# Causal attention, first sequence: keys' parts in tiles of their own, four heads' rows written and two pairs loaded ahead of the rest

## The chip, the cores and the metric

One kernel, one launch, on one core of a Trainium2 chip. The metric is the device time of that launch in microseconds (us), taken as the median over several runs. The time before is 2537.52 us, the median of five runs between 2535.51 and 2549.70 us.

## The reference, cut to what matters

The program is a stack of layers on `x` of shape (4, 1024, 128): a gated linear attention, a mixture of experts, a causal softmax attention, a second mixture of experts, a rotary linear attention with a dense network, a softmax attention with a slope per head ("alibi"), and a dense network again. The change sits in the causal attention:

```
q = (x @ Wq).reshape(B, T, 16, 8).transpose(0, 2, 1, 3)      # B = 4, T = 1024
k = (x @ Wk).reshape(B, T, 16, 8).transpose(0, 2, 1, 3)
v = (x @ Wv).reshape(B, T, 16, 64).transpose(0, 2, 1, 3)
scores = einsum('bhqd,bhkd->bhqk', q, k) / sqrt(8)
scores = where(causal, -inf, scores)
ctx = einsum('bhqk,bhkd->bhqd', softmax(scores), v)
out = ctx.transpose(0, 2, 1, 3).reshape(B, T, 1024) @ Wo
```

`x` has been layer-normed before, and `out` is added to `x`.

## The kernel before

**Pairs.** Heads are worked on two at a time; a sequence has 16 heads, so 8 pairs, and the four sequences have 32. Queries and keys are each split into a high part `hi`, rounded to the matmul's fp32r format, and the remainder `lo`. One product over four copies of the 8 channels (hi.hi, hi.lo, lo.hi, lo.lo) then gives nearly full precision. To bring these copies onto the right partitions they go through device memory: `Pairs.lay_out` writes four copies `a = 0..3` of a whole sequence's queries (`which` 0) or keys (`which` 1) into an image, 16 heads x 8 channels x 1024 positions, 512 KB for each copy (L702). For the queries, copies 0 and 1 are `hi`, 2 and 3 are `lo`; for the keys, 0 and 2 are `hi`, 1 and 3 are `lo`. `Pairs.load` then reads the rows of one pair back, 32 rows of 4 KB for each head, four transfers of 128 KB: two of queries, two of keys (L711). Tiles for six pairs are held. All of these transfers are issued by SyncE (SP), in the order in which they stand in its program. They take one of eight completion semaphores in turn, so that a transfer waits for the eighth before it to have landed.

**Prologue of a sequence** (`prologue(b)`): the experts' result is added to `x`, layer norm, transposes (`xnT`), then for queries and keys in turn: two matmuls of 512 columns into banks of PSUM (L903), a rounding copy to `hi` on ScalarE (L904), the subtraction to `lo` on VectorE (L905), and `lay_out`. `hi` and `lo` are single buffers, so the keys' parts are made in the place of the queries' parts once the queries' rows have left. For the first sequence it also makes the first values `v` (`values`, matmuls L921, copies L927). For later sequences the prologue runs in the middle of the attention of the one before.

**Maxima.** For each pair, `maxima` makes all scores once with the queries stationary (TensorE, L722, `bank<-ca_k,ca_q`; 24 products of 128 to 512 columns) and finds the greatest of each row on VectorE (L750 with the causal mask, L755 without). The maxima are turned (L764), split, and put into the queries' tile as two more rows for each head by small transfers (L772), 8 rows of 512 B each. These pieces are handed out by an iterator `ahead`: 30 pieces, that is two and a half pairs, stand before the first exponential, and later ones are mixed in.

**Main loop** (`softmax_attention`): for two pairs at a time, over blocks of keys: the scores again, with the keys stationary (L722, `scores<-ca_q,ca_k`), the mask added by two small matmuls for each head (`hide`, L728), the exponential on ScalarE (L853) into a tile `e` or, for the first block, `e_first`; then the products with the values (L972, `o<-e,v`), and the sum of exponentials on GpSimd (L990). There is one PSUM buffer for the scores. The tiles `e` are a pool of four buffers of 128 x 1024 words.

**Order.** The order of each engine's instructions is set when the program is built, by a scheduler which works with estimates of its own; on the chip each engine takes its instructions in that order. `alibi_front`, the prologue of the later attention, uses the same `lay_out`; there the rounding copies are L1107 on ScalarE and the subtractions L1108 on GpSimd.

Of the kernel before, what the change touches and what calls it, by code (L numbers as in the profile page):

```python
# [13 lines left out]
F32 = mybir.dt.float32  # L14
I32 = mybir.dt.int32
F32R = mybir.dt.float32r
# [4 lines left out]
P = 128  # L21
B, T = 4, 1024
NB = T // P
NT = B * NB
H = 16
DK = P // H
# [612 lines left out]
class Pairs:  # L639
# [54 lines left out]
            base=512 - P, channel_multiplier=1,  # L694
        )

    def lay_out(self, b, which, hi, lo):

        rows = self.images[b % 2][which][:, self.at :, :].rearrange("h (d a) t -> h d a t", a=4)
        for a in range(4):  # L700
            part = (lo if a >= 2 else hi) if which == 0 else (lo if a % 2 else hi)
            self.k.nc.sync.dma_start(rows[:, :, a, :], part.bitcast(F32))  # L702

    def load(self, n):

# [80 lines left out]
def softmax_attention(  # L786
    k: Core, pairs: Pairs, work, ps_e, scale, maxima, prologue, consume, hold, beside, before=lambda b: None,
    begun=False,
):

    nc = k.nc
    per = H // 2
    count = B * per

    def all_maxima():  # L800
        finish = None
        for n in range(count):
            pieces = maxima(n)
            next(pieces)
            yield
            if finish is not None:
                finish()
            finish = yield from pieces
        finish()

    ahead = all_maxima()
    later = deque()

    def some(n=1):
        for _ in range(min(n, len(later))):
            later.popleft()()

    turn = 0

    if not begun:  # L820
        prologue(0)
        for n in range(4):
            pairs.load(n)

    for _ in range(len(BY_QUERY) * 2 + 6):
        next(ahead, None)
    late = None
    for first in range(0, count, 2):
        if first % per == 0 and first // per + 1 < B:
            before(first // per + 1)  # L830
        if first % per == 2 and first // per + 1 < B:
            prologue(first // per + 1)
        for n in (first + 4, first + 5):
            if n < count:
                pairs.load(n)
        for c, j in BY_KEY:
            start = max(j * P, c * 512)
            w = (c + 1) * 512 - start
            es = []
            for i in range(2):  # L840
                n = first + i
                ps = ps_e.tile([P, 2, 512], F32, tag="scores", name="scores")
                for g in range(2):
                    pairs.product(
                        ps[:, g, :w], n, g, slice(start, start + w), slice(j * P, (j + 1) * P), "k", True,
                        j < 4 * c,
                    )
                if j >= 4 * c:
                    for g in range(2):
                        pairs.hide(ps[:, g, :P], g)  # L850
                tag = "e_first" if hold and j == 0 else "e"
                e = work.tile([P, 2, 512], F32, tag=tag, name=tag)
                power = nc.scalar.activation(e[:, :, :w], ps[:, :, :w], AF.Exp, scale=scale)  # L853
                k.mark = [power.ins.name]
                es.append(e)
                next(ahead, None)
                if late is not None:
                    later.extend(late[i]() or ())
                some()
                turn += 1  # L860
                if beside and turn % 3 == 0:
                    beside.popleft()()
            late = consume(first // per, first % per // 2, c, j, es)
    for part in late:
        later.extend(part() or ())
    some(len(later))
    while beside:
        beside.popleft()()
    next(ahead, None)


def causal_attention(k: Core, pairs: Pairs, wq_d, wk_d, wv_d, wo_d, bring, after):
# [5 lines left out]
    with (  # L878
# [14 lines left out]
        def prologue(b):  # L893
            got.pop()()
            xnT = k.normed(two, b, 1)
            normal[b] = xnT
            for which, w in enumerate((wq, wk)):
                hi = two.tile([P, T], F32R, tag="hi", name="hi", bufs=1)
                lo = two.tile([P, T], F32R, tag="lo", name="lo", bufs=1)
                for c in range(2):  # L900
                    cut = slice(c * 512, (c + 1) * 512)
                    ps = k.bank()
                    nc.tensor.matmul(ps, lhsT=w, rhs=xnT[:, cut], start=True, stop=True)  # L903
                    nc.scalar.copy(hi[:, cut], ps)  # L904
                    nc.vector.tensor_sub(lo[:, cut], ps, hi[:, cut].bitcast(F32))  # L905
                pairs.lay_out(b, which, hi, lo)
            if b == 0:
                for piece in values(b, 0):
                    piece()

# [2 lines left out]
        def values(b, r):  # L913

            v = two.tile([P, NB, 4, dv], F32, tag="v", name="v")
            held[b, r] = v

            def piece(t):
                ps = k.bank()
                for i in range(2):  # L920
                    nc.tensor.matmul(  # L921
                        ps[:, i * 256 : (i + 1) * 256],
                        lhsT=normal[b][:, (t + i) * P : (t + i + 1) * P],
                        rhs=wv[:, r * 256 : (r + 1) * 256],
                        start=True, stop=True,
                    )
                nc.scalar.copy(v[:, t : t + 2].rearrange("p t h d -> p (t h d)"), ps)  # L927

            return [partial(piece, t) for t in range(0, NB, 2)]
# [27 lines left out]
        def consume(b, r, c, j, es):  # L957
# [68 lines left out]
            return first, second  # L1026

        softmax_attention(
            k, pairs, work, ps_e, 1.0 / math.sqrt(DK), partial(pairs.maxima, pool=two, steps=BY_QUERY),
            prologue, consume, True, beside, lambda b: got.append(bring(two, b, "got")),  # L1030
        )

# [93 lines left out]
def alibi_attention(k: Core, pairs: Pairs, weights: AlibiWeights):  # L1126
# [3 lines left out]
    with (  # L1130
# [54 lines left out]
        def consume(b, r, c, j, es):  # L1185
# [53 lines left out]
            return lambda: None, second  # L1239

        softmax_attention(
            k, pairs, work, ps_e, 1.0, partial(pairs.maxima, pool=two, steps=BY_QUERY), prologue, consume,
            False, deque(), begun=True,
# [538 lines left out]
```

## Time and profile before

| | |
|---|---|
| median of five runs | 2537.52 us (2535.51 to 2549.70) |
| the profiled execution's own time | 2543.76 us |
| its span | 2542.0 us |
| mean granted TensorE clock | 0.919 |
| TensorE busy | 2250.7 us, 89% of the span |
| VectorE, ScalarE, GpSimd busy | 1663.7, 1252.6, 926.9 us |
| causal attention | from about 296 to about 1190 us |
| first prologue: addition of the experts' result to first product for the maxima | 300.22 to 331.96 us |

The page has shares of the whole span. For one place in it the order of time has to be read: the timeline gives a start, a duration, engine, line, operation and output and input tiles, a count of merged instructions, and in brackets the idle time before and what ended it. The windows give, for a stretch of time, the busy time of each engine with its count of instructions, then the granted TensorE clock, the busy share of the 16 DMA engines, and GB/s. A matmul in fp32 is recorded twice.

### The profile page before, as it was taken

To read this page: it belongs to the slowest core of one execution; us is meant where nothing else is said; L and a number is where in the kernel's file an instruction comes from. 1 tells how busy PE (TensorE), PEld (TensorE's weight loads), DVE (VectorE), ACT (ScalarE), POOL (GpSimd) and SP (SyncE) were. 2 spreads that over 40 slices of the span, in tenths; PEclk is the share of its full clock that TensorE was granted. 3 is DMA by queue.
4 is the path that set the end of the run, shared out by engine and by line. 5 is a ranking of instruction groups with operands and counts; after the bars stand their busy time and mean duration, and the time that the engine had idled before them with its cause. 6 is when DMAs were issued, how large, how long until landed. Compare 5 with 4: busy or idle time off the path is not lost. (4 is left out here: it accounts for less than half of the span.)

```text
span 2542.0 us, 39865 instructions
## 1 busy us (share of the span) xinstructions
PE 2250.7 (89%) x14101; PEld 1237.2 (49%) x14101; DVE 1663.7 (65%) x4795; ACT 1252.6 (49%) x2033; POOL 926.9 (36%) x722
## 2 busy tenths in 40 slices
PE   6885679999999999998985999989999999997998
PEld 4564533443434344443343666744445444444666
DVE  6978265767657765776434776477777767774544
ACT  6553214455444544553431566615555555556865
POOL 2213405677488748766762333311001000000222
PEclk8987769999889989998997999957999999998999
DMA  9300330200200120100033000402113131000000
GB/s 256 111 9 17 88 103 22 80 19 26 84 26 19 35 83 20 35 19 27 2 101 96 9 9 1 132 2 89 41 28 111 38 97 45 24 24 1 9 9 18
DMA packets 92391, 124.80 MB, mean 49 GB/s; under 512 B 13211, under 2 KB 66462, under 8 KB 92174
## 3 DMA queue, kind: packets, MB, share of 16 engines
q1 hardware_dynamic: 88862, 115.76, 16.2%
q0 software_dynamic: 2560, 5.30, 0.6%
q8 instruction: 120, 1.97, 0.3%
q10 hardware_dynamic: 752, 0.98, 0.1%
q14 instruction: 97, 0.79, 0.1%
HBM read 67.57 MB, written 52.85 MB: 47 GB/s over the span
## 5 line engine op out<-in xcount | busy, mean ns | idle before, releaser
L853 ACT ACTIVATE e<-scores 128x1024 f32<-128x1024 f32 (+3 forms) x704 | 544.8, 792 | 580.0 <-PE scores L728 289.0
L990 POOL TENSOR_TENSOR e_first<-e_first,e 128x1024 f32<-128x1024 f32 (+3 forms) x320 | 540.7, 1718 | 326.1 <-ACT e L853 260.5
L750 DVE CUSTOM_DVE_ANT_0 junk<-bank,mask 128x128 f32<-128x128 f32 (+3 forms) x1024 | 497.3, 486 | 200.4 <-PE bank L722 131.2
L755 DVE TENSOR_REDUCE nm<-bank 128x1 f32<-128x512 f32 x512 | 330.4, 681 | 146.8 <-PE bank L722 144.6
L972 PE MATMUL o<-e,v 128*32 128x512 f32 (+3 forms) x2560 | 305.0, 497 | 0.0
L722 PE MATMUL bank<-aa_k,aa_q 62*128 62x512 f32 (+3 forms) x768 | 245.1, 426 | 25.7 <-DVE nm L755 15.6
L722 PE MATMUL bank<-ca_k,ca_q 62*128 62x512 f32 (+3 forms) x768 | 190.8, 419 | 30.6 <-DMA ca_k<-ca_k 13.9
L1198 PE MATMUL o<-e,v 128*32 128x512 f32 (+3 forms) x1536 | 216.6, 512 | 0.0
L722 PE MATMUL scores<-ca_q,ca_k 64*128 64x512 f32 (+3 forms) x768 | 181.4, 444 | 28.4 <-ACT e L853 26.5
L722 PEld LDWEIGHTS scores<-ca_q,ca_k 64*128 64x128 f32 x768 | 78.2, 188 | 250.4 <-ACT e L853 158.6
L728 PE MATMUL scores<-halves 64*128 64x128 f32 x2048 | 198.8, 260 | 0.0
L728 PEld LDWEIGHTS scores<-halves 64*128 64x128 f32 x2048 | 191.8, 194 | 11.0 <-issue 3.9
L722 PE MATMUL scores<-aa_q,aa_k 64*128 64x512 f32 (+3 forms) x768 | 170.3, 411 | 4.9 <-ACT e L853 4.7
L722 PEld LDWEIGHTS bank<-aa_k,aa_q 62*128 62x128 f32 x768 | 119.1, 198 | 108.2 <-DVE nm L755 60.3
L1108 POOL TENSOR_TENSOR lo<-val,hi 128x512 fp32r<-128x512 f32 x16 | 20.2, 1277 | 388.6 <-ACT hi L1107 369.2
L1516 DVE TENSOR_TENSOR h<-val,h 128x512 fp32r<-128x512 f32 x128 | 90.9, 718 | 102.8 <-ACT h L1515 77.1
L1470 PE MATMUL bank<-h,ff_h1s 128*128 128x512 f32 x512 | 135.5, 409 | 15.4 <-POOL h L1464 10.5
L1460 POOL CAST h<-gate 128x512 fp32r<-128x512 f32 x32 | 26.6, 832 | 335.1 <-DVE gate L1493 325.5
L722 PEld LDWEIGHTS scores<-aa_q,aa_k 64*128 64x128 f32 x768 | 79.6, 190 | 137.9 <-ACT e L853 63.8
L1010 DVE RECIPROCAL raw<-raw 128x128 f32<-128x128 f32 x128 | 117.6, 936 | 44.2 <-ACT raw L1006 44.2
L722 PEld LDWEIGHTS bank<-ca_k,ca_q 62*128 62x128 f32 x768 | 94.7, 200 | 99.1 <-issue 39.2
L1510 ACT ACTIVATE val<-bank,ff_t 128x512 f32<-128x512 f32 x128 | 88.0, 689 | 84.5 <-PE bank L1470 74.6
(291 smaller groups left out, 3719.9 us busy)
## 6 DMA issues: line engine op xcount, KB each, us to landing
aa_q<-aa_q SPq DMA_DIRECT2D x64, 208.0 KB
ca_q<-ca_q SPq DMA_DIRECT2D x64, 128.0 KB
ca_k<-ca_k SPq DMA_DIRECT2D x64, 128.0 KB
aa_k<-aa_k SPq DMA_DIRECT2D x64, 128.0 KB
wi<-in_moe_wi_dram SPq DMA_DIRECT2D x16, 256.0 KB
wo<-in_moe_wo_dram SPq DMA_DIRECT2D x16, 256.0 KB
back<-blank SPq DMA_DIRECT2D x8, 512.0 KB
got<-back SPq DMA_DIRECT2D x8, 512.0 KB
```

The costliest lines, as they stand in the source:

```text
L722: self.k.nc.tensor.matmul(out, lhsT=lhsT, rhs=rhs, start=True, stop=stop, skip_group_check=True)
L728: self.k.nc.tensor.matmul(ps, lhsT=part[:, 0, :], rhs=part[:, 1, :], start=False, stop=(a == 1), skip_group_check=True,)
L750: nc.vector.tensor_tensor_reduce(junk[:, :cols], ps[:, :cols], self.mask[:, 512 - cols :], -1.0, 3e38, ALU.add, ALU.min, to,)
L755: nc.vector.tensor_reduce(to, ps[:, :cols], AX.X, ALU.max, negate=True)
L853: power = nc.scalar.activation(e[:, :, :w], ps[:, :, :w], AF.Exp, scale=scale)
L972: nc.tensor.matmul(outs[which][32 * i : 32 * i + 32, skip:], lhsT=v[:, j, i, 32 * which : 32 * which + 32], rhs=es[i // 2][:, i % 2, : 512 ...
L990: nc.gpsimd.tensor_add(to, to, es[i][:, :, : 512 - skip])
L1010: nc.vector.reciprocal(part, part)
L1198: nc.tensor.matmul(o[32 * i : 32 * i + 32, skip:], lhsT=v[:, j, 4 * r + i, :], rhs=es[i // 2][:, i % 2, : 512 - skip], start=(j == 0), sto ...
L1470: nc.tensor.matmul(ps, lhsT=weights[:, c, :], rhs=inputs[c][i], start=(s == 0), stop=(s == len(steps) - 1))
L1510: nc.scalar.activation(val, ps, AF.Gelu, scale=s[:, o : o + 1])
L1516: nc.vector.tensor_sub(nxt[1][:, o, :], val, hi.bitcast(F32))
```

## The change

For the first sequence, the keys' parts `hi` and `lo` are put into two tiles of the pool of exponentials instead of the buffers that hold the queries' parts. `lay_out` takes a range of heads. For the first sequence it is called four times: heads 0 to 3 of the queries, of the keys; then pairs 0 and 1 are loaded; then heads 4 to 15 of the queries and of the keys; then pairs 2 and 3 are loaded. The loads move from `softmax_attention` into the prologue, in front of the first values. And for the queries' copies, in every sequence and in both attentions, the order of writing becomes 0, 2, 1, 3 (`hi`, `lo`, `hi`, `lo`) instead of 0, 1, 2, 3.

```
-    def lay_out(self, b, which, hi, lo):
-        rows = self.images[b % 2][which][:, self.at :, :].rearrange("h (d a) t -> h d a t", a=4)
-        for a in range(4):
+    def lay_out(self, b, which, hi, lo, heads=slice(0, H)):
+        rows = self.images[b % 2][which][heads, self.at :, :].rearrange("h (d a) t -> h d a t", a=4)
+        of = slice(heads.start * DK, heads.stop * DK)
+        for a in (0, 1, 2, 3) if which else (0, 2, 1, 3):
             part = (lo if a >= 2 else hi) if which == 0 else (lo if a % 2 else hi)
-            self.k.nc.sync.dma_start(rows[:, :, a, :], part.bitcast(F32))
+            self.k.nc.sync.dma_start(rows[:, :, a, :], part.bitcast(F32)[of, :])
...
     if not begun:
         prologue(0)
-        for n in range(4):
-            pairs.load(n)
...
+            laid = []
             for which, w in enumerate((wq, wk)):
-                hi = two.tile([P, T], F32R, tag="hi", name="hi", bufs=1)
-                lo = two.tile([P, T], F32R, tag="lo", name="lo", bufs=1)
+                if b == 0 and which:
+                    hi, lo = (
+                        work.tile([P, 2, 512], F32, tag="e", name="e").bitcast(F32R).rearrange("p g q -> p (g q)")
+                        for _ in range(2)
+                    )
+                else:
+                    hi = two.tile([P, T], F32R, tag="hi", name="hi", bufs=1)
+                    lo = two.tile([P, T], F32R, tag="lo", name="lo", bufs=1)
...
-                pairs.lay_out(b, which, hi, lo)
+                if b:
+                    pairs.lay_out(b, which, hi, lo)
+                laid.append((which, hi, lo))
             if b == 0:
+                for part in laid:
+                    pairs.lay_out(b, *part, slice(0, 4))
+                for n in range(2):
+                    pairs.load(n)
+                for part in laid:
+                    pairs.lay_out(b, *part, slice(4, H))
+                for n in range(2, 4):
+                    pairs.load(n)
                 for piece in values(b, 0):
                     piece()
```

The built program's order changes with it. SP issues eight transfers of 128 KB, the loads of pairs 0 and 1, eight transfers of 384 KB, the loads of pairs 2 and 3. On ScalarE the keys' rounding copies stand before the copies of `v`. On TensorE the first scores (pair 0) and the first products with the values, which stood among the maxima of pairs 1 and 2, stand at the end of pair 2's maxima and behind them; some two hundred instructions on, both orders have done the same work. In the alibi attention's later prologues the keys' rounding copies stand one exponential later on ScalarE.

## Prediction

> **What bounds the kernel now.** The page's first part puts TensorE (PE) at 89% of the span, so time is lost where PE stands still or runs slowly. The change works on one such place, the start of the causal attention. Its timeline comes first (start, duration, engine, line, operation, tiles, count, idle time before and what ended it); lines of PE, ScalarE (ACT), VectorE (DVE) and SP's queue:
>
> ```profile
> 313.48 1.28 SPq L702 DMA_DIRECT2D ca_q<-hi  x2
> 314.80 3.06 SPq L702 DMA_DIRECT2D ca_q<-lo  x2
> ...
> 319.28 1.07 ACT L904 CAST hi<-bank 128x512 fp32r<-128x512 f32 x2 [0.57 <-DMA ca_q<-hi]
> 320.37 1.16 SPq L702 DMA_DIRECT2D ca_k<-hi  x2
> 322.43 1.29 DVE L905 TENSOR_TENSOR lo<-bank,hi 128x512 fp32r<-128x512 f32 x2 [8.25 <-DMA ca_q<-lo]
> 323.75 1.16 SPq L702 DMA_DIRECT2D ca_k<-lo  x2
> 325.11 2.69 SPq L711 DMA_DIRECT2D ca_q<-ca_q  x2
> 329.59 0.77 SPq L711 DMA_DIRECT2D ca_k<-ca_k  x2
> ...
> 331.96 7.44 PE L722 MATMUL bank<-ca_k,ca_q 62*128 62x128 f32 x14 [13.88 <-DMA ca_k<-ca_k]
> ```
>
> The keys' parts wait for the queries' buffers, the keys' load waits for the last row written, and PE waits 13.88 us. This is what the change attacks. The second view is the windows (length; busy us and count of PE, PEld, DVE, ACT, POOL; then granted clock, DMA share, GB/s): first a stretch of the writing, then the idle stretch and what follows.
>
> ```profile
> 315.00:319.00 4.00, 3.08 (x14) 2.12 (x13) 0.00 (x0) 2.34 (x4) 0.00 (x0) 1.00 1.00 333
> ```
>
> ```profile
> 318.20:331.95 13.75, 0.00 (x0) 0.02 (x1) 1.29 (x2) 1.58 (x3) 0.00 (x0) 0.67 0.85 275
> 331.95:366.80 34.85, 31.42 (x70) 16.22 (x72) 29.10 (x101) 2.82 (x4) 0.00 (x0) 0.50 0.21 58
> 366.80:376.70 9.90, 8.82 (x35) 3.84 (x31) 7.41 (x23) 1.61 (x3) 0.00 (x0) 0.98 0.19 55
> 376.70:404.00 27.30, 27.30 (x164) 10.02 (x163) 12.69 (x37) 12.05 (x19) 11.70 (x8) 1.00 0.01 1
> ```
>
> The idle stretch costs twice: PE stands, and its clock then stays at 0.50 for the 35 us of the first maxima, in which DVE (29.10 busy) and the slow PE (31.42) share the pace. From 376.7 on PE has no gap at all, so whatever work is pushed behind that point adds to the end. The third view is the DMA's packets, in a stretch in which the four 512 KB queries' writes landed, and one in which two of the 8-row writes of L772 landed:
>
> ```profile
> DMA packets 665, 2.46 MB, mean 241 GB/s; under 512 B 64, under 2 KB 64, under 8 KB 665
> ```
>
> ```profile
> DMA packets 32, 0.01 MB, mean 3 GB/s; under 512 B 16, under 2 KB 32, under 8 KB 32
> ```
>
> Besides the data there are 64 tiny packets for four writes whose outermost count is 16 heads, so 16 each; and 16 for two writes of 8 rows, so 8 each. I read them as one closing packet for each DMA engine that took part: the outermost count, up to 16, sets how many share a write. A write of four heads would then use four engines.
>
> **The first rows (gain).** The first product for the maxima needs the queries' and keys' rows of pair 0. Both parts of the keys are now ready early: the keys' matmuls end at 314.55, two casts of 0.58 and two subtractions of 0.69 follow, about 316. SP puts out eight writes of 128 KB, 1.05 MB. Their speed is not in the trace, so I bound it. With all 16 engines at 333 GB/s they take 3.1 us, less than their issue: eight at about 0.6 (1.16 for two) from 313.48 give 318.3, plus some 2 us to land. The keys' load then needs, as before, 331.96 - 329.59 = 2.37 us: first product at 322.7, a gain of 9.2 us. With four engines, one engine moves 333/16 = 20.8 GB/s on average and 450/16 = 28 in the best slice (450 GB/s) of the same stretch, so four move 83 to 112 GB/s, and the eight take 9.4 to 12.6 us from the first bytes at about 314.6: 324.0 to 327.2, plus 0.3 to close and 2.37, first product at 326.7 to 329.9, a gain of 2.1 to 5.3. A row four times shorter on a quarter of the engines is no quicker; what is left is that the keys' rows no longer stop for the buffers. I take four engines, as 16 and 8 closing packets lie on that line, and the middle: 3.7 us.
>
> The Trainium skill ("DMA: Bandwidth & Descriptors", section "Why a DMA increments its semaphore by 16 and not by 1") speaks against this change in the same way: the number of engines is the largest up to 16 that divides the slowest dimension of both sides, which makes 4 for four heads and 12 for twelve. At that page's 27 GiB/s for each engine the eight writes would take 9.0 us, an estimate, and the gain would be 5.7.
>
> **The other rows (hidden).** Twelve heads, 3.1 MB: at 12 engines of 20.8 GB/s, 12.6 us; SP reaches them after pair 1's loads, near 329, so they land near 342 and pairs 2 and 3 near 346. Pair 2 is needed after two pairs of maxima, 14.6 us each (331.96 to 346.5), that is near 357; the cover is 11 us, and without it each late us is lost whole. Queued behind them on SP are the L772 rows of pair 0, ready near 343; their first reader now stands at the end of pair 2's maxima, near 369. The keys' copies take two of four `e` tiles; the first `e` that follows the `e_first` tiles comes later still. Nothing of this is paid.
>
> **The new order on PE (loss).** Four `o` products (recorded 8 times, 2.1 us at full clock: 1.04 and 1.06 at 394.57) and the scores and masks of pair 1's first block (about 1.2 us) leave the DVE-bound maxima and go behind pair 2, where PE has no gap. The maxima go a little quicker without them, but the clock stays low longer: in the row above it came back after PE had run unbroken from 363.6, where those very products begin. In the new order the first dense stretch is the values' products and scores at the end of pair 2, some 41 us after the first product instead of 34.85. Work to the common point at 404, in us of full clock: 31.42 x 0.50 + 8.82 x 0.98 + 27.30 = 51.6. After: 41 us, 87% busy at half clock, do 17.8; the other 33.8 at the 97% of the later rows take 34.8; together 75.8 against 72.05, a loss of 3.8. If the clock returns at the old 34.85 with PE 78% busy, 13.6 are done and 39.2 left: 74.0, a loss of 2.0. At 46 us and 85%, 19.6 and 33.0: 79.0, a loss of 7.0. Could it be a gain? Only if the clock never fell. It fell at 322 to 323, some 4.5 us after the last product; the new gap is 8 us or more with four engines, 4.6 with sixteen. In that last case the maxima could go down to DVE's 29.1, 5.8 us less.
>
> The Trainium skill ("TensorE: Matmul & The Clock Gate", the table of its two states) has the clock back after about 3.4 us of sustained work; here PE was 90% busy for 35 us at 0.50, so the row decides. By the page the loss would be near 1 us, an estimate.
>
> **The order hi, lo, hi, lo (small).** The queries' second `hi` write leaves one write later, 1.57 us (512 KB at 333 GB/s), and the keys' cast waits for it. For the causal sequences 1 to 3 the cast had no DMA wait (448.32, issue at 442.23): 0 to 1 each. In the alibi attention three casts waited 3.5 us in all for `aa_q<-hi`; the first, in the dense layer, keeps its place and may pay 1.6, the others stand one exponential of 1.02 later, which covers most. The last `lo` stays fourth, so L1108 waits as long. Behind a waiting cast are exponentials and, through the scores' buffers, PE. Bounds -1 (a cast that no longer holds up an exponential) to +5; I take +1.2.
>
> **Sum.** -3.7 + 3.8 + 1.2 = +1.3 us. The profiled execution took 2543.76 (span 2542.0), so it would be 2545; the median of the runs lies 6.2 below it, so the forecast is 2538.8, rounded 2539.
>
> **Rivals.** (1) The writes use all engines: -9.2, the order costs 2.0 to 3.8, casts +1.2: -6.0 to -4.2, 2531.5 to 2533; with the clock kept up another 5.8, 2526. For it: 275 GB/s in the idle stretch shows what 16 engines do. Against: the closing packets. (2) Slower: the clock. While PE is at 0.50 and bound by itself, each further us costs half a us. If it returns only 58 us after the first product, as it ignored 35 us at 90% before, the loss is 7.0 + 12 x 0.5 = 13, and the sum -3.7 + 13 + 1.2 = +10.5: 2548. From about 62 us on it passes 0.5%. For it: the length of the 0.50 row. Against: the dense work from 363.6 brought it back within 4 us. (3) The casts of the later prologues hold up PE at the upper bound: -3.7 + 3.8 + 5 = +5, 2542.6. (4) The change does not do what it says: the four heads' writes are so slow (each packet twice as long) that the first product comes later than 331.96: 25 us of writing, 342.3, a loss of 10.3, sum +15, 2553.
>
> **How the numbers follow.** A measurement of this kernel can tell about 0.5%, 12.7 us, from no change: 2524.8 to 2550.2. Chances: forecast 0.52 (2533 to 2545), rival 1 0.17, rival 2 0.16, rival 3 0.10, rival 4 0.05. Of rival 1 0.06 fall below 2524.8 with the scatter of the runs; of rival 2 0.08 and of rival 4 0.04 above 2550.2, and of the others 0.03, since before's own runs scatter to 2549.7. So faster 0.06, same 0.79, slower 0.15. The range takes in rival 1 and most of rival 2: 2527 to 2552.
>
> **What would show it.** In the profile after: first product L722 at 326.7 to 329.9 (322.7: rival 1; past 332: rival 4); 4 and 12 closing packets for each write; DMA share near 0.25 while the first eight run; no idle time for DMA at L904 and L905 in the first prologue; clock 0.50 until 41 to 46 us after the first product; ACT waiting for `aa_q<-hi` at L1107 under 6 us. I am wrong if the attention's later part, with the same order, changes its length by more than a few us.

## The result and the profile after

The changed kernel takes 2550.61 us (median of 32 runs, 2539.59 to 2561.46) against 2540.12 us for the kernel before in runs beside it (median of 58, 2523.16 to 2549.7). The ratio is 1.0045 with a 95% interval of 1.0033 to 1.0057: slower by 0.45%, some 11 us, where 2539.0 us and +1.3 us were forecast. It is inside the range and inside the half per cent called "no change", but the interval leaves no doubt of the sign. The profiled execution has a span of 2549.2 us and an own time of 2550.92 us; before, they were 2542.0 and 2543.76. The new lines of code move the numbers: L722 is now L723, L702 is L703, L711 is L712, L904 is L912, L1107 is L1126.

The timeline of the changed kernel at the start of the causal attention (start, duration, engine or queue, line, operation, tiles, count, idle time before and what ended it):

```profile
313.74 0.77 SPq L703 DMA_DIRECT2D ca_q<-hi  x1
...
313.99 0.59 ACT L912 CAST e<-bank 128x512 fp32r<-128x512 f32 x1 [0.27 <-PE bank L911]
...
315.91 0.59 SPq L703 DMA_DIRECT2D ca_q<-lo  x1
316.61 3.65 SPq L703 DMA_DIRECT2D ca_k<-e  x4
321.44 1.35 SPq L712 DMA_DIRECT2D ca_q<-ca_q  x2
326.50 0.77 SPq L712 DMA_DIRECT2D ca_k<-ca_k  x2
...
329.04 2.08 PE L723 MATMUL bank<-ca_k,ca_q 62*128 62x128 f32 x6 [10.77 <-DMA ca_k<-ca_k]
329.16 0.82 SPq L703 DMA_DIRECT2D ca_q<-hi  x1
```

The keys' cast now waits for TensorE and for no DMA. The keys' load is issued at 326.50 instead of 329.59, and PE starts at 329.04. Counted from each kernel's first cast of the queries (311.96 after, 311.19 before), the first product comes after 17.08 us instead of 20.77: 3.7 us sooner.

The windows of the changed kernel: the idle stretch, the stretch until the clock came back, and the next 20.8 us (length; busy us and count of PE, PEld, DVE, ACT, POOL; granted clock, DMA share, GB/s):

```profile
318.10:329.05 10.95, 0.18 (x2) 0.04 (x1) 0.00 (x0) 0.59 (x1) 0.00 (x0) 0.71 0.41 132
329.05:380.20 51.15, 46.68 (x101) 23.93 (x103) 38.85 (x132) 4.47 (x7) 0.00 (x0) 0.50 0.36 111
380.20:401.00 20.80, 20.74 (x145) 8.79 (x144) 7.65 (x23) 9.74 (x15) 7.62 (x6) 0.99 0.01 2
```

The idle stretch is 2.8 us shorter, but PE now runs 51 us at half clock where it ran 35.

The packets of the changed kernel, first from 314.0 to 321.5, in which four of the 128 KB writes landed (0.63 MB with what else was under way), then from 330.5 to 342.0, in which seven and a half of the 384 KB writes did:

```profile
DMA packets 170, 0.63 MB, mean 84 GB/s; under 512 B 16, under 2 KB 16, under 8 KB 170
```

```profile
DMA packets 797, 2.88 MB, mean 250 GB/s; under 512 B 95, under 2 KB 95, under 8 KB 797
```

Sixteen small packets for four writes and 95 for about eight: four engines for four heads, twelve for twelve.

So the start of the attention went much as forecast, and the loss has to be looked for elsewhere: the new order of the queries' rows also holds for every later sequence and for the alibi attention.

### The profile page after: what moved, and what is told of

Read it like the earlier page. It is cut to its first block, busy times and chain, and to the rows that moved or that the text cites. A ratio compares the mean times of both kernels' runs of the same rounds, so it can differ in the third digit from the quotient of the medians.

```text
span 2549.2 us, 39870 instructions
## 1 busy us (share of the span) xinstructions
PE 2258.0 (89%) x14101; PEld 1239.4 (49%) x14101; DVE 1666.4 (65%) x4795; ACT 1253.5 (49%) x2033; POOL 929.2 (36%) x722
## 5 line engine op out<-in xcount | busy, mean ns | idle before, releaser
L991 PE MATMUL o<-e,v 128*32 128x512 f32 (+3 forms) x2560 | 308.0, 493 | 0.0
L723 PE MATMUL bank<-aa_k,aa_q 62*128 62x512 f32 (+3 forms) x768 | 245.4, 430 | 25.5 <-DVE nm L756 15.3
L1217 PE MATMUL o<-e,v 128*32 128x512 f32 (+3 forms) x1536 | 219.1, 516 | 0.0
L723 PE MATMUL bank<-ca_k,ca_q 62*128 62x512 f32 (+3 forms) x768 | 193.7, 420 | 27.5 <-DVE nm L756 11.2
L723 PE MATMUL scores<-ca_q,ca_k 64*128 64x512 f32 (+3 forms) x768 | 179.6, 441 | 31.4 <-ACT e L853 29.5
L723 PEld LDWEIGHTS scores<-ca_q,ca_k 64*128 64x128 f32 x768 | 76.7, 186 | 254.6 <-ACT e L853 161.7
L723 PE MATMUL scores<-aa_q,aa_k 64*128 64x512 f32 (+3 forms) x768 | 172.9, 418 | 4.2 <-ACT e L853 4.1
L723 PEld LDWEIGHTS bank<-aa_k,aa_q 62*128 62x128 f32 x768 | 119.9, 200 | 110.3 <-DVE nm L756 60.5
L723 PEld LDWEIGHTS scores<-aa_q,aa_k 64*128 64x128 f32 x768 | 81.1, 194 | 137.0 <-ACT e L853 63.7
L723 PEld LDWEIGHTS bank<-ca_k,ca_q 62*128 62x128 f32 x768 | 95.9, 200 | 95.2 <-issue 35.0
L1529 ACT ACTIVATE val<-bank,ff_t 128x512 f32<-128x512 f32 x128 | 88.1, 689 | 86.5 <-PE bank L1489 76.4
```

Source lines behind the costliest of these rows:

```text
L723: self.k.nc.tensor.matmul(out, lhsT=lhsT, rhs=rhs, start=True, stop=stop, skip_group_check=True)
L991: nc.tensor.matmul(outs[which][32 * i : 32 * i + 32, skip:], lhsT=v[:, j, i, 32 * which : 32 * which + 32], rhs=es[i // 2][:, i % 2, : 512 ...
L1217: nc.tensor.matmul(o[32 * i : 32 * i + 32, skip:], lhsT=v[:, j, 4 * r + i, :], rhs=es[i // 2][:, i % 2, : 512 - skip], start=(j == 0), sto ...
L1529: nc.scalar.activation(val, ps, AF.Gelu, scale=s[:, o : o + 1])
```

## Experiments

Each was timed in five rounds beside the kernel before on the same chip; a ratio is to that kernel, with its 95% interval. `order_only` rests on six executions, the others on twelve.

**The new order alone, and the change without it.** First edit, to the kernel before; second, to the changed kernel:

```
# order_only, on the kernel before
-        for a in range(4):
+        for a in (0, 1, 2, 3) if which else (0, 2, 1, 3):
# no_order, on the changed kernel
-        for a in (0, 1, 2, 3) if which else (0, 2, 1, 3):
+        for a in range(4):
```

> Only the order hi, lo, hi, lo of the queries' copies, in all sequences of both attentions; the first sequence otherwise as before. Theory A (the first sequence costs about 3 us net, the rest of the 11 us comes from the order of the copies, which moves instructions in the later prologues): +5 to +9 us. Theory B (all 11 us come from the first sequence's new order of TensorE, clock included): 0, within 2 us. First product for the maxima at the same place as before, 331.9 us, in both.

> The whole change but for the order of the copies, which stays hi, hi, lo, lo. Its TensorE order differs from before in the first sequence's start alone. Theory A: +2 to +4 us against before. Theory B: +9 to +12 us. In both the first product for the maxima stands near 328.5 us, 3 us earlier than before.

Measured: the order alone 1.0075 [1.0046, 1.0104], 2555.41 us; the change without the order 1.0005 [0.9988, 1.0022], 2539.75 us. The split of the first sequence is worth nothing that these runs can tell (its interval is -3 to +6 us), as its two terms of the sum had it; the order alone costs at least as much as the whole change, and more than the +5 to +9 us expected. What the changed kernel pays for it is the gap between 1.0045 and 1.0005, some 10 us, give or take 5.

**The keys' tiles alone.** The keys' parts in two `e` tiles, but all 16 heads written at once and all four pairs loaded behind them:

```
# keys_only, on the kernel before
+                if b == 0 and which:
+                    hi, lo = (work.tile([P, 2, 512], F32, tag="e", name="e")... for _ in range(2))
...
                 pairs.lay_out(b, which, hi, lo)
```

> Only the keys' parts of the first sequence in two tiles of the pool of exponentials; rows of all 16 heads written at once, loads as before, TensorE's order the same as before. The writes run without the stop for the buffers: eight of 512 KB at 333 GB/s from 314.6 us, 12.6 us, and 2.7 us to the first product: 329.9 us, 2.1 us earlier than before. As no instruction of TensorE changes place, both theories have the gain kept: -1 to -3 us in the whole.

Measured: 0.9999 [0.9977, 1.002]; the 1 to 3 us expected are too small for these runs to show. The first product came 19.41 us after the first cast instead of 20.77: of the 3.7 us, 1.4 come from the tiles and the rest from writing less ahead of it.

**The same split on all 16 engines.** With an image that has no unused row (in all causal sequences), heads and rows are one outermost dimension of 128 or 384; `self.first` is then 0:

```
# sixteen, on the changed kernel
-            pairs = Pairs(k, rows, Pairs.room(dram, "ca", 1), "ca", 6, 1)
+            pairs = Pairs(k, rows, Pairs.room(dram, "ca", 0), "ca", 6, 1)
...
+            to = rows[:, :, a, :]
+            if not self.first:
+                to = to.rearrange("h d t -> (h d) t")
...
```

> The whole change, and the causal images in device memory without their unused extra row, so that heads and channels are one dimension and a write of four heads goes out over 32 rows. The order of TensorE and ScalarE is that of the changed kernel. Theory of four engines: these writes leave 16 closing packets instead of 4, the eight take under 5 us, and the first product stands at 322.7 us, 6 us earlier than in the changed kernel; the whole is 4 to 7 us shorter than the changed kernel. Rival (the four heads' writes were slow for another reason, such as their 32 partitions): first product at 329 us as in the changed kernel, and the same time.

Measured: 1.0025 [1.0008, 1.0041]. From 313 to 321 us its trace has 158 packets under 512 B for eight writes and the first two loads, so nearly 16 each. Its timeline (same columns as above):

```profile
316.15 1.91 SPq L707 DMA_DIRECT2D ca_k<-e  x4
318.59 0.79 SPq L716 DMA_DIRECT2D ca_q<-ca_q  x2
320.87 0.77 SPq L716 DMA_DIRECT2D ca_k<-ca_k  x2
...
323.51 2.08 PE L727 MATMUL bank<-ca_k,ca_q 62*128 62x128 f32 x6 [4.89 <-DMA ca_k<-ca_k]
```

The first product comes 11.65 us after the first cast, 9.1 sooner than before; the forecast's first rival had 9.2 for that case. Of these 9.1 us only 3.0 are left at exponential 80 (all counts of exponentials start at 0; 244.35 us after the first cast, against 247.30 before): the clock came back 47.8 us after the first product instead of 35.3. It is still slower than the kernel before, by the order that it also carries.

**Where the order costs.** The order in one attention only:

```
# order_causal, on the kernel before
+        for a in range(4) if self.by_head or which else (0, 2, 1, 3):
# order_alibi, on the kernel before
+        for a in (0, 2, 1, 3) if self.by_head and not which else range(4):
```

> The kernel before with the queries' rows written hi, lo, hi, lo in the causal attention only; the alibi attention writes hi, hi, lo, lo as before. The order alone in both attentions cost 1.0075 [1.0046, 1.0104], that is 12 to 26 us. Theory A (the cost lies in the alibi attention, whose casts of the keys stand in ScalarE's queue behind the wait and whose built order changes on ScalarE in 47 lines against 16): within 4 us of the kernel before, 2534 to 2542. Theory B (the cost lies in the causal attention, where the built order changes on TensorE in 141 lines against 35): 10 us or more over the kernel before. Theory C (it is spread evenly over all later sequences): some 5 to 10 us.

> The kernel before with the queries' rows written hi, lo, hi, lo in the alibi attention only; the causal attention writes them as before. Theory A: 10 us or more over the kernel before. Theory B: within 4 us of it. Theory C: some 5 to 10 us. Its cost and that of the causal attention alone should add up to the 12 to 26 us of both if the two do not act on each other.

Measured: causal alone 1.0039 [1.0012, 1.0066], alibi alone 1.0021 [1.0, 1.0041]. The two add up to 1.0060, against 1.0075 for both. The even spread (C) fits best. The intervals, some 3 to 17 us and 0 to 10 us, do not by themselves rule out that most of it lies in one of the two; the profiles further down have a loss in both.

**Is it the wait for the buffer, or the order of the writes?** Three runs:

```
# order_rest, on the kernel before: the new order, except in the causal attention's first sequence
+        for a in (0, 1, 2, 3) if which or not (b or self.by_head) else (0, 2, 1, 3):
# after_first, on the changed kernel: the new order in that sequence alone
+        for a in (0, 1, 2, 3) if which or b or self.by_head else (0, 2, 1, 3):
# alibi_two, on order_alibi: two buffers for the parts (of the three later sequences; the first has tiles elsewhere)
-        hi = pool.tile([P, T], F32R, tag="hi", name="hi", bufs=1)
-        lo = pool.tile([P, T], F32R, tag="lo", name="lo", bufs=1)
+        hi = pool.tile([P, T], F32R, tag="hi", name="hi", bufs=2)
+        lo = pool.tile([P, T], F32R, tag="lo", name="lo", bufs=2)
```

> The kernel before with the queries' rows written hi, lo, hi, lo everywhere but in the causal attention's first sequence, so exactly where the changed kernel's keys still share the buffers of the queries' parts. Theory A (the order costs only where the keys' casts wait for those buffers): the gap between the changed kernel and the one with its order undone, 1.0045 less 1.0005, so 1.004 or 8 to 12 us over the kernel before. Theory B (most of the cost of the order comes from the first sequence, as its keys stand in the way of the first product there): within 4 us of the kernel before. The order in all sequences cost 1.0075, so by theory A some 7 us of that were the first sequence's and do not exist in the changed kernel.

> The changed kernel with the new order in the first sequence alone, where the keys' parts lie in tiles of their own and wait for no write; all later sequences write hi, hi, lo, lo. Theory A: the same as the changed kernel with the order undone everywhere, 1.0005, so 0.999 to 1.002 of the kernel before. If the interleaved order costs as such, by the way in which it reaches memory: 1.002 to 1.005.

> The kernel with hi, lo, hi, lo in the alibi attention alone, which cost 1.0021 [1.0, 1.0041], and two buffers each for the hi and lo parts of its later three sequences, so that the keys' casts there wait for no write of the queries; its first sequence, prepared beside the dense layer, keeps one. Theory A: the cost goes, 0.998 to 1.001. If the cost lies in the first sequence beside the dense layer, or in the writes themselves: still 1.001 to 1.004.

Measured: order_rest 1.0037 [1.0021, 1.0054], after_first 1.0002 [0.9984, 1.002], alibi_two 0.9991 [0.9975, 1.0007]. Where the keys share the buffers, the order costs what the changed kernel lost (1.0037 beside the gap of 1.0040). Where they don't, the same order of writes shows no cost: in the first sequence of the changed kernel, whose instructions on PE, DVE, ACT and POOL are then the same as without it, and in the alibi attention once the buffers are two. So the dependence of the keys' casts on the queries' buffer costs, not the order in which the rows reach memory. For the first sequence this is shown. For the alibi attention there is a gap: two buffers without the order were not run on the kernel before, and in the last experiment below they go with another 0.9984 to 0.9961, so part of what alibi_two regains may be their own gain. In the later causal sequences two buffers were not tried. That order_only is at 1.0075 and order_rest at 1.0037 would leave some 10 us to the first sequence, but their traces speak against it: all instructions on PE, DVE, ACT and POOL stand in the same order in both, only one write on SP has another place, and at exponential 80 they are 0.6 us apart (248.38 and 247.75; before, 247.30). The intervals touch, so scatter is the likelier reading; it is not shown.

The waits of the keys' casts in the alibi attention, in the changed kernel and then in the one with two buffers (us, times):

```profile
L1126 ACT CAST hi<-val x16: 601/619/622, 1594.2 to 2088.9; 128x512 fp32r<-128x512 f32 x16
...
  DMA aa_q<-hi: 4.1, 2
```

```profile
L1107 ACT CAST hi<-val x16: 610/618/622, 1583.4 to 2069.8; 128x512 fp32r<-128x512 f32 x16
...
  DVE val L1104: 9.5, 8
  DVE val L1106: 6.3, 6
```

With two buffers no cast waits for DMA. But in the changed kernel it is only 4.1 us, against 3.5 before: this wait itself can't be the 10 us.

**A later release still.** The queries' rows as lo, lo, hi, hi, so that the keys' first cast waits for the fourth write:

```
# lohi, on the kernel before
+        for a in (0, 1, 2, 3) if which else (2, 3, 0, 1):
```

> The kernel before with the queries' rows written lo, lo, hi, hi, in both attentions. The keys' first cast then waits for the fourth write instead of the second; in the order hi, lo, hi, lo it waits for the third. Theory A (the later release of the buffer costs, directly or by the instruction order that is built around it): slower than before by at least what hi, lo, hi, lo cost, 1.0075 or 19 us, and up to twice that. If the interleaving of the two parts is what costs: within 4 us of the kernel before, as the writes of a part stand together here.

Measured: 1.0032 [1.0014, 1.005]. It is slower, so the interleaving is not what costs, but not by more than hi, lo, hi, lo. The expectation of 19 us or more missed: the alibi casts now wait 7.3 us for `aa_q<-hi`, against 4.1 and 3.5, and the cost did not grow with it.

**Where the time goes.** Line up the exponentials of all kernels by their number, 96 for each sequence of the causal attention, and compare the time between two of them. Over the alibi attention, from its exponential 0 to 383, the five with the order there and one buffer take 625.2 to 629.6 us, the eight others 618.4 to 624.1 (lohi, in neither, 631.6). Most of this is one stretch of its first sequence, from exponential 16 to 48. In the five (the changed one, order_only, order_alibi, order_rest, sixteen) it takes 65.8 to 66.2 us. In seven of the eight others, which write hi, hi, lo, lo there or have two buffers, it takes 61.1 to 61.9; the eighth, the profiled execution of the kernel before, took 65.8 (lohi 63.3). Its windows in the changed kernel, from where the clock falls, and then in no_order (columns as above):

```profile
1766.50:1790.40 23.90, 22.53 (x110) 11.55 (x110) 16.28 (x55) 15.78 (x22) 2.75 (x3) 0.50 0.47 151
1790.40:1811.30 20.90, 20.19 (x151) 9.73 (x151) 14.20 (x49) 9.35 (x14) 0.00 (x0) 1.00 0.11 27
```

```profile
1752.60:1759.40 6.80, 5.92 (x28) 3.37 (x27) 4.57 (x17) 6.74 (x10) 2.49 (x2) 0.50 0.64 209
1759.40:1790.50 31.10, 29.82 (x228) 14.70 (x226) 23.00 (x80) 16.40 (x25) 0.00 (x0) 1.00 0.22 63
```

Apart from the end of a stall PE is busy in both; what differs is the clock. It falls in both at the same 2.9 us stall of PE (for `nm` from DVE), changed kernel first:

```profile
1767.78 0.58 PE L723 MATMUL bank<-aa_k,aa_q 62*128 62x256 f32 x1 [2.90 <-DVE nm L756]
```

```profile
1751.72 0.38 PE L723 MATMUL bank<-aa_k,aa_q 62*128 62x256 f32 x1 [2.90 <-DVE nm L756]
```

Without the order it is back after 6.8 us, with it after 23.9. ScalarE's timeline behind the stall, in the changed kernel:

```profile
1768.33 1.94 ACT L853 ACTIVATE e<-scores 128x1024 f32<-128x1024 f32 x2
1770.15 0.59 ACT L1225 COPY o_sb<-o 128x512 f32<-128x512 f32 x1
1770.76 1.28 ACT L109 ACT_TABLE_LOAD   x1
1772.06 0.21 ACT L109 ACTIVATE ln_r<-ln_ve 128x4 f32<-128x4 f32 x1
1772.17 1.12 ACT L1126 CAST hi<-val 128x512 fp32r<-128x512 f32 x2
1773.31 1.28 ACT L853 ACT_TABLE_LOAD   x1
1774.60 1.51 ACT L853 ACTIVATE e<-scores 128x768 f32<-128x768 f32 x2
```

and in no_order:

```profile
1752.27 1.02 ACT L853 ACTIVATE e<-scores 128x1024 f32<-128x1024 f32 x1
1753.19 1.13 ACT L1126 CAST hi<-val 128x512 fp32r<-128x512 f32 x2
1754.21 1.03 ACT L853 ACTIVATE e<-scores 128x1024 f32<-128x1024 f32 x1
1755.13 0.59 ACT L1225 COPY o_sb<-o 128x512 f32<-128x512 f32 x1
1755.59 0.83 ACT L853 ACTIVATE e<-scores 128x768 f32<-128x768 f32 x1
1756.44 1.28 ACT L109 ACT_TABLE_LOAD   x1
```

The casts were put later when the program was built, and with them the rest was reshuffled: the first exponential of 768 columns, which frees the next scores, now stands behind two table loads and the casts, 6.3 us after the first exponential where it was 3.3. On PE the products for the maxima are bunched into this gap (2.65 us of them in a row from 1775.20) and leave the scores for later. ScalarE and PE show no wait for DMA here: the cost goes with the built order, and with a clock that does not come back in it.

How the one makes the other is not shown. All five kernels with the order stayed at 0.50 for 23.89 us, the others for 6.83 to 10.24, but the kernel before for 23.89 with the same order on ScalarE as no_order. Where the fall lies against the stall differs between executions and matters, but does not explain it all: no_order is one of three in which the clock fell 0.9 us after the stall's end, and these three have the 6.83; where it fell 0.3 to 1.3 us ahead of the stall's end, two kernels without the order (after_first, keys_only) had 10.24, the kernel before and the five with the order 23.89. Nor are the two table loads enough: in alibi_two the exponential of 768 columns also stands behind two, 5.2 us after the first, and the clock was back after 10.24 us.

In the causal attention the same comparison (exponentials 120 to 150, the end of the second sequence's prologue) gives 91.0 to 95.4 us with the order and 86.5 to 94.4 without, 93.7 against 90.4 in the mean of five and of eight. Single executions overlap there, so this part, 3 us, is likely rather than shown. In the alibi attention the means over all its exponentials are 626.6 and 620.7, 6 us; together that makes 9 of the 10.

**A version that beats both.** First the split on 16 engines without the order, then with two buffers for the parts in the alibi attention:

```
# sixteen_no_order: sixteen, with  for a in range(4):
# best: sixteen_no_order, and in the alibi attention
-        hi = pool.tile([P, T], F32R, tag="hi", name="hi", bufs=1)
-        lo = pool.tile([P, T], F32R, tag="lo", name="lo", bufs=1)
+        hi = pool.tile([P, T], F32R, tag="hi", name="hi", bufs=2)
+        lo = pool.tile([P, T], F32R, tag="lo", name="lo", bufs=2)
```

> The changed kernel with hi, hi, lo, lo as before the change, and with an image without its unused row, so that heads and rows are one outer dimension of 128 or 384 and a write is shared by all 16 engines. If the gains and losses add: the changed kernel is 1.0045, without the new order 1.0005, with sixteen engines 1.0025, so this one 0.9985, some 4 us under the kernel before (2531 to 2537). If the earlier first product is lost to a clock that stays low, as the first step of the forecast says of part of it: within 2 us of the kernel before.

> The two edits that helped, together: sixteen engines for the first writes with the order hi, hi, lo, lo (0.9984 [0.9966, 1.0003]), and two buffers each for the hi and lo parts of the alibi attention's later sequences (with the order hi, lo, hi, lo they brought 1.0021 down to 0.9991). If the two add, some 4 us from the first and 0 to 2 us from the second, as the order hi, hi, lo, lo left little wait to remove: 2531 to 2536, or 0.997 to 0.999 of the kernel before. If the second edit only takes away what the order had cost: as the first alone, 0.998 to 1.000.

Measured: sixteen_no_order 0.9984 [0.9966, 1.0003], 2536.45 us; best 0.9961 [0.9946, 0.9976], 2529.86 us, the only one whose interval lies below the kernel before, by 10 us. It is a little under the 0.997 expected; the intervals of the two touch, so what the second buffer adds is not clear of noise.

## Why the prediction was right, and where it was wrong

The measured time lies in the range, near its upper end; the forecast itself, +1.3 us, was short by 10 us, and nearly all of that is one term. That the range holds it is in part luck: its upper end was set for a clock that stays low at the start (rival 2), and the loss came elsewhere.

- **The first rows, -3.7 us.** Right in size and in mechanism: 3.7 us in the changed kernel, 3.2 in the two with other orders later (first product 17.6 us after the first cast), four and twelve engines by the closing packets, DMA share 0.21 from 313.74 to 321.00, while the first eight ran. That the middle of a range of 2.1 to 5.3 was hit to a tenth is luck. Even the alternative held: 9.1 us on 16 engines, 9.2 forecast. The rule of the Trainium skill that was weighed there ("DMA: Bandwidth & Descriptors", section "Why a DMA increments its semaphore by 16 and not by 1") names the right numbers of engines. By its speed the gain would have been 5.7, an estimate, so here the bounds from the rows were the better price.
- **The other rows, hidden.** Right: SP issued the twelve heads from 329.16 to 340.2 and the next pairs until 348.2; nothing on PE waits for them.
- **The new order on PE, +3.8 us (2.0 to 7.0).** Right in mechanism, at the upper end in size. The clock came back 51.6 us after the first product, not after 41 to 46. At exponential 80 the changed kernel is 3.0 us behind the kernel before, the same without the later order 3.7 and after_first 1.2; with the 3.2 to 3.7 us of earlier start that makes a loss of 4.4 to 6.9. The three have the same order on PE here, yet in after_first the clock came back after 42.6 us and in no_order after 51.9: a part of this differs between executions of the same order.
- **The order hi, lo, hi, lo, +1.2 us (-1 to +5).** This is the step that failed. It measured some 10 us (1.0045 less 1.0005; 1.0037 [1.0021, 1.0054] by itself), twice the upper bound. The wait that it priced was sized well: 4.1 us for `aa_q<-hi` after, 3.5 before, and 0.3 us for `ca_q<-hi` in the later causal sequences. It also knew that the keys' casts stand one exponential later in the built order, but counted this only as cover for the wait. What it put at nothing is what moves with them: the changed order on ScalarE and PE goes with a clock that stayed at 0.50 for 23.9 us where it was 6.8 to 10.2 in most others. The rival with the casts (+5 us, 2542.6) was the right place with the same fault. The sign that it named for being wrong, a change in the length of the attention's later part by more than a few us, was too coarse and looked at one attention: from exponential 96 to 383 the causal attention takes 702.0 us in the mean of five with its order and 698.7 in eight without, while the alibi attention changed by 6.
- **Rival 2, the clock (2548).** The nearest number, from 13 us lost at the start by a clock that returns after 58 us; it returned after 51.6. The clock goes with much of the time lost, but at other places: the split of the first sequence alone is neutral (1.0005).

## What to carry to other kernels

A buffer released one write later is not priced by the wait for it: look at what the build moves on the engines behind the waiting instruction, and at every other place that the edited helper serves, because here the one line outside the change's subject cost all of its loss. Where the granted clock falls at a stall, an edit that only regroups the work behind it can go with more lost time than the stall has (4 to 5 us here, behind one of 2.9); compare the granted clock of the same work in both profiles before looking for waits. One profile of each kernel was not enough: the kernel before happened to show the long low stretch as well, and only many kernels lined up by the number of an instruction separated the cases.

## What the runs showed of the hardware

The granted clock changes only on a grid. In all 14 traces the stretches at 0.50 and at 1.00 are multiples of 3.413 us (6.83, 10.24, 23.89, 47.79, 58.03), apart from the last, which the end cuts, and the grid's phase against the kernel differs between executions. Taken over these traces, after a window at full clock with PE busy under 40% the clock always fell (243 of 243), over 70% nearly never (54 of 8017). At half clock it never came back after a window with PE busy under 80% (0 of 556), but after one with PE busy 99.5% or more it came back only 360 times in 591. What in a full window counts was not settled.

The Trainium skill ("TensorE: Matmul & The Clock Gate", section "Part 1: The HAM clock gate (the "warmup" mystery)") has such a free-running window of about 3.4 us, and the return to full clock after one busy window. The window agrees with the 3.413 us here; the return does not always, as in the changed kernel the clock stayed at 0.50 at the stall for seven windows although PE was busy throughout the second.

Much of the scatter from run to run goes with the clock. Over 93 runs of the kernel before time and mean granted clock go together with a correlation of -0.81, 14 us for each 0.01. The mean clock was 0.9250 before and 0.9189 in the changed kernel, worth 8.5 us by that slope, of the 12.4 us between the means of those runs. In order_rest it is less: 0.9235 against 0.9252 in the runs beside it, worth 2.4 of 8.2 us. So that the clock is most of the order's cost is not shown.
